# A graph layer on one core: the norms of the second and third pair of row blocks move by one product, and the first weight quarter is loaded in two parts

## The chip, the core and the metric

The kernel runs on one core of a Trainium2 chip. The metric is device time in microseconds (us), the median of several runs. The engines are named as in the profile: PE is TensorE, which does the matmuls (PEld is its weight load); DVE is VectorE; ACT is ScalarE; POOL is GpSimd; SP is SyncE, which only issues DMAs here. ACT and POOL issue DMAs as well.

## What is computed

The reference normalises each row of x, applies a relu, and runs a relational graph convolution with a highway gate on the result. Cut to what matters:

```python
h = jnp.maximum(_layernorm(x, axis=-1), 0.0)      # x: 1250 x 1024, float32
u = h @ root + bias
for r in range(8):                                # 20000 edges, 8 types
    mean_r = (sum of h[src] over the edges of type r into each row) / max(count, 1)
    u = u + mean_r @ weight[r]                    # 1024 x 1024 each
z = concatenate([u, h], axis=1) @ w_gate + b_gate
out = x + tanh(u) * z + h * (1.0 - z)
```

## The kernel before

**Blocks and steps.** The 1250 rows are ten blocks of 128 (the last has 98). `NP` is 5, and blocks i and i + 5 form pair i. The kernel multiplies h with all eight `weight[r]`, with `root` and with the two halves of `w_gate`, and gathers the products row by row later. A step (s, i) multiplies pair i with matrix s. Steps run over i inside s.

**A step is seven products.** A pair has 2 x 2 quarters of the left side (A11, A12 from the first block, A21, A22 from the second), and the matrix has 2 x 2 quarters of 512 x 512 (`b11`, `t3` at first, `b21`, `b22`). The step uses Winograd's form of Strassen's scheme with seven products. `left` makes the sums S1, S2, S4 and S3 on DVE, and `make_t1` to `make_t4` (L167, L171, L175, L179) make the right sides, also on DVE. Each product is four `k`-blocks of 128 rows, in float32, which the profile shows as eight matmuls of L292. For the first matrix the order of the products is A11, S1, S2, S4 (`p3`), S3 (`p7`), A12 (`p2`), A22, except in the step (0, 0), where A12 comes directly behind A11. The products use two PSUM banks `b` and `c` in turn. ACT copies them out behind A11 (L330), S1 (L337), S2 (L341, called the sixth product in the code), S3 (L316) and A22 (L359). DVE adds behind S4 (L309), S3 (L317) and A12 (L325). The copies matter for order: S2 and S3 accumulate into the bank that L330 and L341 read, and S4 into the one that L337 reads.

**The norm.** The input of a pair is loaded into SBUF (L560). `both` normalises the two blocks: statistics and scale factors on DVE (L579, L583, L588, L589), a square root on ACT (L584), and the scaled relu on ACT (L605). `store` writes h to DRAM (L610). `with_x` adds x and h on DVE and stores the sum (L615, L616). `factored` and `transposed` then transpose h on PE (L259) and copy the result out on ACT and DVE (L266, L264) to be the left side. The first pair is done ahead of all products in a shorter way (L598, L262); `second_block` does its second half behind the first product.

**Order of the work beside the products.** Every engine works through its instructions in the order in which the program writes them; there is no scheduler that changes it (`manual_schedule`). After each product the kernel calls `done()`, which calls `between`, which advances a generator `index()` by one `yield`. So a `yield` more or less moves all that follows in the generator by one product, on all engines. `index()` runs `norms()` and `columns()` side by side, one `yield` each per product, with `norms()` first. `columns()` makes the edges' keys on DVE (L709 to L721 behind the seventh product, L728 to L741 one product later), and transposes them on PE (L748, L749). When both have ended, `slots` gives each edge its place in a table, in 40 chunks of two `yield`s (small matmuls L802 and L853 on PE, L784 and L786 on ACT, L807 and others on DVE, scatters L881 on POOL), and `order` sorts the rows and loads the table back (L935 on DVE, L527, L537, L490 on POOL). From step (4, 0) on, `weights` (L513 to L519) and the gathers (L1061, L1069) work with that table.

**Loads.** x and the first matrix are loaded through SP's queue, except the right halves of x's blocks 0 and 5, which go through ACT's queue. The order on SP today is x(0), x(5), `b11`, `b21`, `t3`, `b22` (all L135 but x), then the second and third pair of x. `b11` is 1 MiB.

Of the kernel before, what the change touches and what calls it, by code (L numbers as in the profile page):

```python
# [19 lines left out]
def tile_rgcn_highway(  # L20
# [35 lines left out]
    P = 128  # L56
# [4 lines left out]
    KQ = KC // 2  # L61
    Q = D // 2
# [27 lines left out]
    def nrows(d):  # L90
        return min(P, N - d * P)
# [34 lines left out]
    class Factors:  # L126
# [3 lines left out]
        def __init__(self, w, old=None):  # L130
            self.w, self.old = w, old

        def load(self, i, j, to, queue=None):
            queue = queue or (nc.scalar if self.old else nc.sync)
            queue.dma_start(to, self.w[i * Q:(i + 1) * Q, j * Q:(j + 1) * Q]  # L135
                            .rearrange("(k p) n -> p k n", p=P))
            return to

        def load_first(self):
            old = self.old  # L140
            if old is None:
                free = wbuf
                self.place = dict(b11=free[0], t3=free[1], b22=free[2], t1=free[3], t2=free[4],
                                  b21=free[5], t4=free[6])
                self.spare = free[7:]
            else:
                p = old.place
                self.place = dict(b11=old.spare[0], t3=old.spare[1], b22=p["b11"], t1=p["t1"],
                                  t2=p["t2"], b21=p["b22"], t4=p["t3"])
                self.spare = [p["b21"], p["t4"]]  # L150
            p = self.place
            self.of = {A11: p["b11"], A12: p["b21"], S4: p["b22"], S1: p["t1"], S2: p["t2"],
                       S3: p["t3"], A22: p["t4"]}
            self.load(0, 0, p["b11"])

        def load_next(self):
            self.load(0, 1, self.place["t3"], nc.sync)
# [23 lines left out]
    class Second:  # L181
# [22 lines left out]
        def left(self):  # L204
            nc.vector.tensor_add(self.s1, self.a21, self.a22)
            nc.vector.tensor_sub(self.s2, self.s1, self.a11)
            nc.vector.tensor_sub(self.s3, self.a11, self.a21)
            nc.vector.tensor_sub(self.s4, self.a12, self.s2)
# [43 lines left out]
    def transposed(aop, part, of, n, relu=False):  # L252


        for half, to in enumerate(((A11, A12), (A21, A22))[part]):
            p = bank().rearrange("p (k f) -> p k f", k=KQ)
            for i in range(KQ):
                k = KQ * half + i
                nc.tensor.transpose(p[:, i, :n], of[:n, k * P:(k + 1) * P], ident[:n, :n])  # L259
            to_n, p_n = aop[:, to, :, :n], p[:, :, :n]  # L260
            if half and relu:
                nc.vector.tensor_scalar_max(to_n, p_n, 0.0)  # L262
            elif half:
                nc.vector.tensor_copy(to_n, p_n)  # L264
            else:
                nc.scalar.activation(to_n, p_n, AF.Relu if relu else AF.Copy)  # L266
            if n < P:
                nc.gpsimd.memset(aop[:, to, :, n:], 0.0)
# [103 lines left out]
    fac = []  # L372
# [173 lines left out]
    with ExitStack() as early:  # L546
# [6 lines left out]
        def load_x(i, part, t=None, pieces=1):  # L553
            d = i + part * NP
            n = nrows(d)
            if t is None:
                t = xpool.tile([P, D], F32, name="xt")
            for j in range(pieces):
                at = slice(j * D // pieces, (j + 1) * D // pieces)
                (nc.scalar if j else nc.sync).dma_start(t[:n, at], x[d * P:d * P + n, at])  # L560
            return t

        def scratch(i, part):

            return h_op[i][:, 2 * part:2 * part + 2].rearrange("p a k f -> p (a k f)")
# [52 lines left out]
        def both(a, b):  # L618

            a.stats(0)  # L620
            a.stats(1)
            a.spread()
            b.stats(0)
            a.scale()
            a.relu()
            b.stats(1)
            b.spread()
            b.scale()
            b.relu()

        def factored(i, blocks):
            for part in range(2):
                transposed(h_op[i], part, blocks[part].ht, blocks[part].n)


        warm = xpool.tile([P, 1], F32, name="warm")
        x0 = [load_x(0, part, pieces=2) for part in range(2)]
        nc.scalar.activation(warm, eps, AF.Sqrt)
        fac[0].load_first()
        fac[0].load_b21()  # L640
        fac[0].load_next()
        fac[0].load_b22()
# [307 lines left out]
                    yield  # L950

        def norms():
            yield
            yield
            both(*b1)
            fac[0].make_t4()
            for b in b1:
                b.store()
            yield
            yield  # L960
            yield
            factored(1, b1)
            left(h_op[1])
            yield
            for b in b0:
                b.with_x()
            x3 = [load_x(3, part) for part in range(2)]
            b2 = [Normed(2 + part * NP, x2[part], scratch(NP - 1, part)) for part in range(2)]
            both(*b2)
            yield  # L970
            for b in b2:
                b.store()
            yield
            for b in b1:
                b.with_x()
            yield
            factored(2, b2)
            b2[0].with_x(b2[0].ht)
            b2[1].with_x()
            left(h_op[2])  # L980
            x4 = [load_x(4, 0)]
            yield
            yield
            b3 = [Normed(3 + part * NP, x3[part], scratch(NP - 1, part)) for part in range(2)]
            both(*b3)
            yield
            for b in b3:
                b.store()
            yield
            factored(3, b3)  # L990
            left(h_op[3])
            yield
            for b in b3:
                b.with_x()
            x4.append(load_x(4, 1))
            yield
            for part in range(2):
                ht = xpool.tile([P, D], F32, name="xt") if part else scratch(NP - 1, 1)
                b = Normed(4 + part * NP, x4[part], ht)
                b.stats(0)  # L1000
                b.stats(1)
                b.spread()
                b.scale()
                b.relu()
                b.store()
                yield
                transposed(h_op[4], part, b.ht, b.n)
                b.with_x()
                yield
            left(h_op[4])  # L1010
            first_part.close()
# [11 lines left out]
        while going[0]:  # L1023
            s, i = next(steps)
# [11 lines left out]
    with ExitStack() as edges_part:  # L1036
# [44 lines left out]
        def edges(g, blocks, to, late=0):  # L1081

            of = u_dram[g - 1] if g else None
            nb = len(blocks)
            starts = [late + sum(K[g][d] for d in blocks[:b]) for b in range(nb + 1)]
            leaves = [starts[b + 1] - 1 + GOT for b in range(nb)]
            reads = [max(-1, starts[b] - 5, leaves[b - UB] if b >= UB else -1) for b in range(nb)]  # L1090
            u, then = {}, {}
            for t in range(-1, leaves[-1] + 4):
                for b, d in enumerate(blocks):
                    if starts[b] <= t < starts[b + 1]:
                        k = t - starts[b]
                        add_slot(u[d], g, d, k, idx[:, g], w_of[:, g], first=g == 0 and k == 0)
                for b, d in enumerate(blocks):
                    if t == leaves[b]:
                        then[t + 3] = to(d, u[d])
                if then.get(t):  # L1100
                    then[t]()
                for b, d in enumerate(blocks):
                    if t == reads[b]:
                        u[d] = new_u(d, of, g)
                yield
# [49 lines left out]
        def beside(e, total, s, i, last):  # L1155


            between = spread(e, total, 7 * ((last - s) * NP + NP - i))
            while s <= last:
                step(s, i, between)  # L1160
                s, i = next(steps, (NM, 0))
            return s, i

        s, i = next(steps)
        while s <= R0[1]:
            step(s, i)
            s, i = next(steps)
# [8 lines left out]
        def with_others(e):  # L1176

            others = other_groups()
            for k, _ in enumerate(e):
                yield  # L1180
                if k % 2:
                    next(others, None)
            for _ in others:
                pass

        weights(0)
        s, i = beside(with_others(edges(0, range(ND), u_back(0))), sum(K[0]) + 2, s, i,
                      R0[2] - 1)
# [6 lines left out]
        for g in range(1, G - 1):  # L1195
# [3 lines left out]
            s, i = beside(e, sum(K[g]) + LATE + 1, s, i, R0[g + 2] - 1)  # L1199
# [153 lines left out]
        while s < NM - 1:  # L1353
# [8 lines left out]
            s, i = next(steps, (NM, 0))  # L1362

        for i in range(NP):
# [55 lines left out]
            else:  # L1420
                product(h_op[i % 2], fac[NM - 1], t, between=beside_last, last=finish_last,
                        pieces=2, second=lambda: None,
# [24 lines left out]
```

## Time and profile before

| what | value |
|---|---|
| median of 3 runs | 1368.39 us (1367.49 to 1369.36) |
| the profiled execution's own time | 1366.53 us |
| its span, from first to last instruction | 1364.7 us |
| mean granted TensorE clock | 1.000 |
| busy: PE, DVE, POOL, ACT | 1349.9, 932.9, 638.8, 365.7 us |
| products in float32 (L292) | 2800 matmuls, 593 ns each |

A line of a group of instructions or of the timeline names the engine, the line in the source, the operation, the tiles written and read, and the count; in brackets stands how long the engine was idle before it and which instruction ended that. The view of waits sums the same by pair of waiting and releasing line. A copy that is late does not show as a wait of the copying engine, when that engine was busy with something else: it shows as a wait of PE for that copy.

### The profile page before, as it was taken

Reading aid. Unit: us, or ns where it says so; the run is one execution under the profiler, and the core shown is the slowest. Engines: PE = TensorE matmul, PEld = TensorE weight load, DVE = VectorE, ACT = ScalarE, POOL = GpSimd, SP = SyncE. Lnnn points to the kernel's source line nnn. Section 1 sums busy time; section 2 is a strip of 40 time slices with the busy share of each in tenths; the row PEclk is TensorE's granted clock in tenths of the full one; section 3 lists DMA queues with packets and bytes.
Section 4 is the critical chain, followed back from the end, with each engine's and each line's share of the span. In section 5 each row is a group of like instructions: output and inputs, shape, how many; then the busy total and the mean of one; then the engine's idle time right before and its main releaser. Section 6 shows DMA issues by size and latency. Waiting matters only on the chain.

```text
span 1364.7 us, 12816 instructions
## 1 busy us (share of the span) xinstructions
PE 1349.9 (99%) x3810; PEld 659.9 (48%) x3810; DVE 932.9 (68%) x1849; ACT 365.7 (27%) x792; POOL 638.8 (47%) x571
## 2 busy tenths in 40 slices
PE   8999999999999999999999999999999999999998
PEld 4444455455445544544554454455445445544443
DVE  6855887887885946567565756765664586567985
ACT  3235566566631111111111111111111111121220
POOL 0002655665561464557774435465443344435641
PEclk9999999999999999999999999999999999999999
DMA  8654565855663175379788627787965664586861
GB/s 312 253 196 131 121 139 134 191 115 114 158 167 93 61 206 137 116 250 254 218 282 315 213 81 287 264 303 258 347 217 201 217 239 149 194 284 219 294 205 58
DMA packets 110202, 272.77 MB, mean 200 GB/s; under 512 B 25956, under 2 KB 27986, under 8 KB 110000
## 3 DMA queue, kind: packets, MB, share of 16 engines
q0 software_dynamic: 48912, 128.60, 29.5%
q1 hardware_dynamic: 45088, 111.34, 26.3%
q10 hardware_dynamic: 16128, 31.98, 7.9%
q8 instruction: 30, 0.49, 0.2%
q14 instruction: 44, 0.36, 0.1%
HBM read 214.20 MB, written 80.65 MB: 216 GB/s over the span
## 4 chain that ended last, share of the span: by engine, by line
PE 91%; issue 4%; DVE 2%; POOL 1%; DMA 1%; ACT 0%; SPq 0%; POOLq 0%; DVEq 0%; ACTq 0%
PE ps L292 82%; PE ps L212 8%; PE ps L259 1%; PE ps_n L802 1%; DMA w<-in_L_gnn_weight_dram 1%; POOL out_dram L496 1%; DVE h_op L275 0%; PE ps_q L853 0%; POOL got L490 0%; DMA xt<-in_x_dram 0%; DVE st L579 0%; DMA xh_dram<-xt 0%; DVE h_op L615 0%; DVE w L171 0%; DVE h_op L264 0%
## 5 line engine op out<-in xcount | busy, mean ns | idle before, releaser
L292 PE MATMUL ps<-w,h_op 128*128 128x512 f32 x2800 | 1224.5, 593 | 6.2 <-ACT row L341 2.6
L292 PEld LDWEIGHTS ps<-w,h_op 128*128 128x128 f32 x2800 | 526.6, 190 | 620.2 <-issue 601.5
L1061 POOL DMA_INDIRECT got<-y,idx x202 | 256.0, 1267 | 265.7 <-DVE u L1069 197.2
L1069 DVE SCALAR_TENSOR_TENSOR u<-got,w_of,u 128x1024 f32<-128x1024 f32 (+1 forms) x192 | 246.0, 1283 | 127.6 <-DMA got<-y,idx 125.1
L881 POOL DMA_INDIRECT table<-row_col,at_i x157 | 180.2, 1148 | 154.1 <-DVE at_i L877 73.3
L317 DVE TENSOR_TENSOR row<-row,part 128x512 f32<-128x512 f32 x55 | 38.0, 690 | 109.6 <-ACT part L316 109.6
L359 ACT COPY row<-ps 128x512 f32<-128x512 f32 x50 | 29.3, 585 | 239.0 <-PE ps L292 234.1
L316 ACT COPY part<-ps 128x512 f32<-128x512 f32 x55 | 32.2, 585 | 179.8 <-PE ps L292 176.6
L309 DVE TENSOR_TENSOR row<-row,ps 128x512 f32<-128x512 f32 x54 | 36.9, 684 | 57.3 <-PE ps L292 53.3
L330 ACT COPY row<-ps 128x512 f32<-128x512 f32 x55 | 32.2, 586 | 163.2 <-PE ps L292 163.2
L337 ACT COPY row<-ps 128x512 f32<-128x512 f32 x55 | 32.2, 586 | 147.9 <-PE ps L292 144.3
L212 PE MATMUL ps<-w,w 128*128 128x256 f32 x288 | 71.3, 380 | 0.0
L341 ACT COPY row<-ps 128x512 f32<-128x512 f32 x55 | 32.2, 586 | 139.3 <-PE ps L292 139.3
L212 PEld LDWEIGHTS ps<-w,w 128*128 128x128 f32 x288 | 54.4, 190 | 20.9 <-issue 15.3
L807 DVE TENSOR_TENSOR seen<-seen,ps_n 128x110 f32<-128x110 f32 x157 | 42.1, 268 | 25.1 <-PE ps_n L802 20.8
L867 DVE SCALAR_TENSOR_TENSOR junk<-k_bc,key_col,before 128x128 f32<-128x128 int32 x157 | 54.9, 350 | 4.2
L527 POOL DMA_INDIRECT node_dram<-ids,pos_i x30 | 37.4, 1247 | 43.2 <-issue 42.9
L212 PE MATMUL ps<-w,h_op 128*128 128x256 f32 x216 | 56.0, 382 | 0.0
L935 DVE SCALAR_TENSOR_TENSOR junk<-v_bc,val,one 128x1280 bf16<-128x1280 f32 x30 | 46.6, 1554 | 9.5 <-DMA v_bc<-val_dram 8.7
L212 PEld LDWEIGHTS ps<-w,h_op 128*128 128x128 f32 x216 | 40.5, 190 | 25.3 <-issue 22.2
L784 ACT ACTIVATE is_lo<-io,less_lo 128x128 bf16<-128x128 f32 x157 | 50.1, 391 | 4.8 <-DMA xh_dram<-xt 4.8
L490 POOL DMA_INDIRECT u<-u_dram,node x20 | 22.9, 1145 | 51.3 <-DMA last_dram<-u 34.9
(187 smaller groups left out, 957.8 us busy)
## 6 DMA issues: line engine op xcount, KB each, us to landing
y<-row SPq DMA_DIRECT2D x72, 512.0 KB, 5.6
w<-in_L_gnn_weight_dram ACTq DMA_DIRECT2D x21, 1024.0 KB, 10.1
w<-in_L_gnn_weight_dram SPq DMA_DIRECT2D x11, 1024.0 KB, 13.3
k_bc<-keys_dram SPq DMA_DIRECT2D x39, 256.0 KB, 4.2
l_bc<-los_dram SPq DMA_DIRECT2D x39, 256.0 KB, 8.4
w<-in_L_gnn_w_gate_dram ACTq DMA_DIRECT2D x6, 1024.0 KB
h_dram<-h_op SPq DMA_DIRECT2D x9, 512.0 KB, 2.9
hr_dram<-row SPq DMA_DIRECT2D x9, 512.0 KB, 6.7
```

Source lines behind the costliest of these rows:

```text
L212: nc.tensor.matmul(p, a[:, k, :], b[:, k, :], start=(fresh and k == 0), stop=(k == 1), skip_group_check=True)
L292: nc.tensor.matmul(b[:, at], aop[:, i, k, :], w.of[i][:, k, at], start=(fresh and k == 0), stop=(k == KQ - 1), skip_group_check=True)
L309: nc.vector.tensor_add(c12, c12, c)
L317: nc.vector.tensor_add(c22, c22, d)
L527: ins = nc.gpsimd.indirect_dma_start(out=node_dram[g][:, :], out_offset=bass.IndirectOffsetOnAxis(ap=pos_i[:, g, d:d + 1], axis=0), in_=id ...
L784: nc.scalar.activation(is_lo[:, i, :], io, AF.Abs, bias=less_lo[:, c0 + i:c0 + i + 1])
L807: nc.vector.tensor_add(seen[j][:, i, :], was, p[:, i, :])
L867: nc.vector.scalar_tensor_tensor(junk, o["k_bc"][:, i, :], key_col[:, c:c + 1], before, op0=OP.is_equal, op1=OP.mult, accum_out=rank[:, c: ...
L881: ins = nc.gpsimd.indirect_dma_start(out=table[:, :], out_offset=bass.IndirectOffsetOnAxis(ap=at_i[:n, i:i + 1], axis=0), in_=row_col[:n, ...
L935: nc.vector.scalar_tensor_tensor(junk, v_bc[:, g, :], val[:, c:c + 1], one.to_broadcast([P, KEYS]), op0=OP.is_gt, op1=OP.mult, accum_out=p ...
L1061: nc.gpsimd.indirect_dma_start(out=t[:n], out_offset=None, in_=y[g][:, :], in_offset=bass.IndirectOffsetOnAxis(ap=at[:n, d, k:k + 1], axis=0),
L1069: nc.vector.scalar_tensor_tensor(u[:n], t[:n], w, u[:n], op0=OP.mult, op1=OP.add)
```

## The change

Three edits to the order, none to what is computed. First, `load` and `load_first` get a parameter `k`, and `b11` is loaded in two DMAs of two `k`-blocks each, the first in front of block 5 of x, the second behind it. Second, in `norms()` one `yield` moves from behind the second pair's norm to in front of it, so that it stands behind S2 instead of S1 in step (0, 0). Third, there is one more `yield` behind the first pair's `with_x`, so that the loads of the fourth pair's x and the third pair's norm come behind A11 of step (0, 1), and one more between the norm and the transposes of each block of the last pair. `norms()` has 22 `yield`s instead of 19.

```diff
-        def load(self, i, j, to, queue=None):
+        def load(self, i, j, to, queue=None, k=slice(0, KQ)):
             queue = queue or (nc.scalar if self.old else nc.sync)
-            queue.dma_start(to, self.w[i * Q:(i + 1) * Q, j * Q:(j + 1) * Q]
+            queue.dma_start(to[:, k], self.w[i * Q + k.start * P:i * Q + k.stop * P,
+                                             j * Q:(j + 1) * Q]
                             .rearrange("(k p) n -> p k n", p=P))
...
-        def load_first(self):
+        def load_first(self, k=slice(0, KQ)):
...
-            self.load(0, 0, p["b11"])
+            self.load(0, 0, p["b11"], k=k)
...
-        x0 = [load_x(0, part, pieces=2) for part in range(2)]
+        x0 = [load_x(0, 0, pieces=2)]
+        fac[0].load_first(slice(0, 2))
+        x0.append(load_x(0, 1, pieces=2))
         nc.scalar.activation(warm, eps, AF.Sqrt)
-        fac[0].load_first()
+        fac[0].load(0, 0, fac[0].place["b11"], k=slice(2, KQ))
...
         def norms():
-            yield
-            yield
+            for _ in range(3):
+                yield
             both(*b1)
             fac[0].make_t4()
             for b in b1:
                 b.store()
             yield
             yield
-            yield
             factored(1, b1)
             left(h_op[1])
             yield
             for b in b0:
                 b.with_x()
+            yield
             x3 = [load_x(3, part) for part in range(2)]
             b2 = [Normed(2 + part * NP, x2[part], scratch(NP - 1, part)) for part in range(2)]
             both(*b2)
...
                 b.store()
+                yield
                 yield
                 transposed(h_op[4], part, b.ht, b.n)
                 b.with_x()
```

## The prediction

> **What bounds the kernel now.** I read the page's busy shares first, then TensorE's waits, then the timeline of the first 50 us, where nearly all of these waits lie. All times are those of the profiled execution.
>
> ```profile
> PE 1349.9 (99%) x3810; PEld 659.9 (48%) x3810; DVE 932.9 (68%) x1849; ACT 365.7 (27%) x792; POOL 638.8 (47%) x571
> ```
>
> TensorE is busy 99% of the span, so only what makes it stand still, or gives it more work, can move the time. The view of TensorE's waits (releaser: us in total, times, longest):
>
> ```profile
> PE ps L292 <- ACT row L341: 2.6, 1, 2.6
> PE ps L292 <- ACT row L330: 1.6, 1, 1.6
> ...
> PE ps L292 <- DMA w<-in_L_gnn_weight_dram: 1.3, 1, 1.3
> PE ps L259 <- ACT xt L605: 0.8, 1, 0.8
> ...
> PE ps L748 <- DVE h_op L264: 0.5, 1, 0.5
> ```
>
> Five waits, 6.8 us together, each once. The same view from 130 us to the end has one line, 0.7 us on "issue". So 6.8 us (0.5%) is the most that this change can gain, and the question is which of the five it removes and what it puts there. The timeline (start, duration, then in brackets the idle time before it and its releaser):
>
> ```profile
> 7.46 0.60 ACT L266 ACTIVATE h_op<-ps 128x512 f32<-128x512 f32 x1 [1.59 <-PE ps L259]
> 9.16 3.67 PE L292 MATMUL ps<-w,h_op 128*128 128x512 f32 x8 [1.28 <-DMA w<-in_L_gnn_weight_dram]
> ...
> 13.54 13.90 PE L292 MATMUL ps<-w,h_op 128*128 128x512 f32 x32
> ...
> 14.35 1.22 DVE L167 TENSOR_TENSOR w<-w,w 128x1024 f32<-128x1024 f32 x1
> ...
> 28.19 2.28 DVE L179 TENSOR_TENSOR w<-w,w 128x2048 f32<-128x2048 f32 x1
> 28.31 1.24 ACT L605 ACTIVATE h_op<-h_op,less,rs 128x1024 f32<-128x1024 f32 x1 [0.42 <-DVE less L589]
> ...
> 29.46 0.56 ACT L341 COPY row<-ps 128x512 f32<-128x512 f32 x1
> ...
> 30.08 3.70 PE L292 MATMUL ps<-w,h_op 128*128 128x512 f32 x8 [2.63 <-ACT row L341]
> ...
> 41.36 1.27 DVE L579 BATCH_NORM_STATS2 st<-h_op 128x6 f32<-128x512 f32 x2
> ...
> 46.77 0.56 ACT L330 COPY row<-ps 128x512 f32<-128x512 f32 x1
> ...
> 47.39 2.84 PE L292 MATMUL ps<-w,h_op 128*128 128x512 f32 x6 [1.57 <-ACT row L330]
> ```
>
> See the 2.63 us: the 32 matmuls from 13.54 are A12, S1, S2, S4, 3.44 us each, so S2 ended near 23.9. Its copy L341 stands on ACT behind the second pair's norm, whose last activation ends at 29.5, and S3 needs the bank that L341 reads. The 1.57 us is the same with the third pair's norm in front of L330. The 1.28 us is TensorE waiting for the first quarter `b11` although its left side (L266) was ready at 8.06.
>
> **The change part by part.** I lay out the new order on the old clock.
>
> *Start.* SP's queue becomes x(0), half of b11, x(5), other half. The windows view has 379 to 412 GB/s from 6 us on; all of x(0), x(5) and b11 (2.1 MB) landed at 9.03 (the chain: issue 1.67 plus 7.36). The last half MiB takes 1.3 us of that, x(5)'s SP piece 0.65, so the first half lands near 6.5 to 7, x(5) near 7.3 to 7.6, the second half still near 9.1. A11 then starts when L266 is done, at 8.15 instead of 9.16; its third k-block comes 1.75 us later, at 9.9, so the second half has 0.8 us to spare. Gain: 1.0 us. The price is x(5): its stats (L579) began at 7.03 and would begin up to 0.6 later; its first relu piece (now 9.76 to 10.5) then ends near 11.1, and its transposes are wanted at 11.66: covered. [...] The windows row of this trace:
>
> ```profile
> 8.00:9.00 1.00, 0.00 (x0) 0.00 (x0) 1.00 (x3) 0.06 (x1) 0.00 (x0) 1.00 1.03 397
> ```
>
> In the last microsecond of the wait the engines are full at 397 GB/s with several loads queued. [...] I take the row. [...]
>
> *After A11.* A12 starts at 12.5, S1 could at 15.97. S1 needs the first half of t1 (L167) and its left sum (L275). L167 needs t3, two MiB after b11: 9.03 + 2 x 2.6 (1.05 MB at 404 GB/s), about 14.2. So VectorE starts L167 at 14.2, only 0.15 earlier than now, and S1 starts at 16.05. Then S2 19.5, S4 22.9, S3 26.4.
>
> *Second pair's norm one product later.* VectorE has no instruction between S1 and S2, so its order does not change: stats still from 24.1, t4 (L179) until 30.3. Only ACT changes: L341 now stands before the norm and runs at 23.0 to 23.6, and behind it the issue of the next matrix's first load (0.39 us in this trace), both before the sqrt at 25.65. S3 starts at 26.4 without a wait: the 2.63 us is gone. What is late next: the transposes behind S3 (29.9) need both relus, which end at 27.7 and 29.55; covered by 0.3 to 1.3 us. A22 follows at 31.65 (t4 ready at 30.3) instead of 35.36: 3.7 earlier.
>
> *Third pair's norm in the next step.* Now A11 and L330 of step 1 come before this norm, so L330 is free and the 1.57 us goes. In exchange the norm stands behind `columns()`'s first part on VectorE, and in front of its second part and of L337. VectorE from t4 on, without a pause: L309 and L317 1.2, two transposed copies 1.25, left sums 2.74, L615 twice 2.35, casts and keys L709 to L721 2.5: 40.2 to 40.6. Norm on VectorE 4.23 (41.36 to 45.59 now): 44.4 to 44.8. L728 to L741, 2.74 (48.41 to 51.15 now): tb ready at 47.2 to 47.5. TensorE ends S2 of step 1 at 45.65, and the next instruction in its queue is now the transpose of key, row and tb (L748), because the sixteen transposes of the third pair, which stand before it today, have moved behind S4. Its own work is 1.34 (1.82 less the 0.48 wait), so S4 could start at 47.0, but tb lets it start at 47.7 to 48.05: a new wait of 0.7 to 1.05, in place of 1.57 and 0.48. L337 (after the norm's relus, 40.4 + 5.5 = 45.9, so done by 46.6) is earlier than that and hides. Compare S4's start: now 54.50 with the 1.75 us of transposes before it, that is 52.75; then 47.7 to 48.05: 4.7 to 5.05 gained. VectorE sets this point from 14.2 on, so the 1.0 us of the start is mostly swallowed here.
>
> *The last norm and the rest.* The extra yield puts the last block's transposes behind A11 of step 3, two products after its norm, where ACT's relu (now 87.87 to 89.1) is long done: the 0.85 us goes. The fourth pair's norm now sits after A12, its transposes after the next A11; relus end near 67.4, the second block's transposes stand at 68.0: 0.6 us of cover. Sum: 4.7 to 5.05 plus 0.85, 5.6 us.
>
> *What moves on the queues.* On SP the x(3), x(8) loads fall behind four key stores and two y stores, issued near 42.5 against 43.0 now, and wanted at 62; the next matrix's second load moves ahead of two h stores and is wanted 80 us later; the xh stores stay with L615. `norms` has 22 yields instead of 19, so all slots and the ordering come three products later. ACT's first L784 stays behind the landing of the last xh store (4.8 us idle today, hidden by L342's one product of slack). On POOL the scatters L881 and the chain L527, L537, L490 shift by 3 x 3.6 = 10.8 us against the products: the last idx load at 490.3 is wanted by `weights(0)` at 516.2, and the gathers' first four buffers, issued by 505.5, at 524.9. Both keep over 8 us even with some landing time; without that cover each us over would hold VectorE and then TensorE. The index part now ends in step (3, 4) instead of (3, 3), still before step 4. TensorE's instructions are the same, so I cost them at nothing.
>
> Unknown: how the slots' small matmuls fall between the products after a shift by an odd number of products. From one side, 40 chunks (157 columns of edges by four) with no wait in some 300 us today: nothing. From the other, weight loads waiting for L786 0.2 us four times: if each chunk did so, 8 us lost; in favour, up to 0.7 ("issue"). I take nothing, the nearer row: two products per chunk and seven per step bring either alignment in the kernel of today as well.
>
> The profiled execution took 1366.53 (span 1364.7), 1.9 below the median; taking 5.6 off gives 1360.9 on that execution and 1368.39 - 5.6 = 1362.8 for the median.
>
> **The rivals.** *The wait comes back (chance 0.14).* Norm, columns and transposes meet on VectorE between 30 and 48 us. For it: VectorE is busy throughout and L337 waits for the norm. If this stretch runs 2.5 us longer than added up, S4 starts at 50.4 and the gain is 3.1: 1365.3; about half of this case falls within 0.2%. Against: every term is a measured duration.
>
> *The slots lose step (0.10): slower.* L802 and L853 wait for ACT's L786 and L837 at the new alignment. From 5.6/40 = 0.14 us per chunk the gain is gone, from 0.21 it is slower by over 0.2%; at 0.3 it is 12 us: 1374.8. For: VectorE and ACT are more than half full there. Against: no such wait today.
>
> *It does not do what it says (0.04).* If S3 were really held by another releaser than L341 and the split bought nothing: 1368.4. Against: the copy starts within 0.1 us of the norm's last relu ending, and S3 within 0.1 us of the copy's end.
>
> **How the numbers follow.** Likeliest (0.72): 1362.8, on its own 1361.3 (all waits gone, 6.8) to 1364.5. The range goes to 1367.0, so that it holds most of the first rival, and down to 1361.0. 0.2%, 2.7 us, is about what a measurement of this kernel can tell from no change. Faster by more: 0.72 and half of 0.14, with a little for tails: 0.80; same: 0.10; slower: 0.10.
>
> **What would show it.** Right: A11 starts near 8.2; no wait on L341, L330 or L605; a new wait of about 1 us on TensorE at L748 for VectorE's row or tb; S4 of step 1 near 48; still none after 130. Wrong: A11's third block waiting for its half; the x(5) transposes waiting; a wait on L337; waits at L802 or L853; w_of waiting for idx near 511.

## The result, and the profile after

| | before | after |
|---|---|---|
| median of 7 runs, same chip | 1368.39 us (1367.49 to 1369.90) | 1364.05 us (1362.83 to 1364.52) |
| ratio, 95% interval | | 0.9965 (0.9954 to 0.9977) |
| profiled execution, its span | 1366.53, 1364.7 us | 1364.05, 1362.3 us |

The change made the kernel 4.3 us (0.35%) faster; 1362.8 was forecast. Two later comparisons gave 7.8 and 5.9 us for the same two kernels; what makes these differ is taken up below. One execution, of the kernel with the filled hole, ran at about half the clock throughout (mean clock 0.556, 2410 us) and is left out of that kernel's median. Lines of the source are a few higher after the change (L292 is L293, L341 is L342, L748 is L751).

First the busy shares of the page of after, then its view of TensorE's waits (waiting line, releaser: us in total, times, longest):

```profile
PE 1350.3 (99%) x3810; PEld 659.9 (48%) x3810; DVE 932.0 (68%) x1849; ACT 365.4 (27%) x792; POOL 639.8 (47%) x571
```

```profile
PE ps_q L856 <- ACT s_b L840: 1.4, 1, 1.4
...
PE ps L293 <- ACT row L342: 1.0, 1, 1.0
PE ps L751 <- DVE row L742: 0.9, 1, 0.9
PE ps L293 <- issue: 0.7, 1, 0.7
PE ps L260 <- DVE h_op L599: 0.7, 1, 0.7
...
```

TensorE has the same 3810 instructions. Of the five waits that the prediction listed none is left. In their place stands the 0.9 us on L742. The first and the 1.0 us line are new too, and they lie elsewhere: L342 here is at 180 us and L840 at 358 us, in the slots part (the expectations below put the latter near 405 us). The timeline of the start, TensorE alone (start, duration, in brackets the idle time before it and its releaser):

```profile
8.28 3.70 PE L293 MATMUL ps<-w,h_op 128*128 128x512 f32 x8 [0.23 <-ACT h_op L267]
12.04 1.36 PE L260 MATMUL ps<-ident,h_op 128*128 128x128 f32 x8
13.24 17.62 PE L293 MATMUL ps<-w,h_op 128*128 128x512 f32 x40
30.70 1.91 PE L260 MATMUL ps<-ident,h_op 128*128 128x128 f32 x16
32.45 13.90 PE L293 MATMUL ps<-w,h_op 128*128 128x512 f32 x32
...
47.49 0.33 PE L751 MATMUL ps<-ident,row 128*128 128x128 f32 x1 [0.86 <-DVE row L742]
...
48.35 3.70 PE L293 MATMUL ps<-w,h_op 128*128 128x512 f32 x8
```

Where 32 matmuls stood before the 2.63 us hole, 40 now run without one (13.24: A12, S1, S2, S4, S3), and S4 of step (0, 1) starts at 48.35. The same stretch on VectorE and ScalarE:

```profile
8.43 1.28 DVE L580 BATCH_NORM_STATS2 st<-xt 128x6 f32<-128x512 f32 x2 [1.15 <-DMA xt<-in_x_dram]
...
14.92 1.22 DVE L168 TENSOR_TENSOR w<-w,w 128x1024 f32<-128x1024 f32 x1 [0.79 <-DMA w<-in_L_gnn_weight_dram]
...
24.04 0.59 ACT L342 COPY row<-ps 128x512 f32<-128x512 f32 x1 [2.85 <-PE ps L293]
...
47.01 0.43 DVE L742 TENSOR_TENSOR row<-row,late 128x256 f32<-128x256 f32 x1
```

L342 runs at 24.04, before the norm instead of behind it. But L168 now has an idle 0.79 us in front of it, released by a DMA; in the profile before it started at 14.35 with no wait.

Where the gain is kept and lost is best seen by counting. All kernels have the same 2800 large matmuls in nearly the same order, so the start of the n-th one in before (counted from 0), less its start in another kernel, is the gain up to there (both from the traces):

```
n-th matmul   at (before)    after   after on the chip of the third comparison
    48          35 us         2.9      2.9
   176         100 us         5.5      5.5
   300         156 us         5.9      5.8
   400         210 us         5.0      6.1
   700         363 us         3.1      5.8
  1000         506 us         2.45     5.2
 2799 (last)  1359 us         2.45     5.2
```

The rows between 176 and 1000 need care. The small matmuls of the slots (L805 and L856) begin behind the 183rd large one in before and three products later in after, so at 300 after has done eight of them fewer, worth 0.4 us, and does them by the end of the slots. At 176 and at 1000 both kernels have done the same work. So the change earned 5.5 us in the first 100 us, as worked out, and in the profiled execution on record 3.1 of it was lost again by 506 us: 0.25 on the third chip as well, and 2.8 with the two late waits (2.4 of it listed as idle time).

### The profile page after: what moved, and what is told of

It is laid out like the page before. It is cut to its first block, busy times and chain, and to the rows that moved or that the text cites. A ratio compares the mean times of both kernels' runs of the same rounds, so it can differ in the third digit from the quotient of the medians.

```text
span 1362.3 us, 12814 instructions
## 1 busy us (share of the span) xinstructions
PE 1350.3 (99%) x3810; PEld 659.9 (48%) x3810; DVE 932.0 (68%) x1849; ACT 365.4 (27%) x792; POOL 639.8 (47%) x571
## 4 chain that ended last, share of the span: by engine, by line
PE 90%; issue 4%; DVE 2%; DMA 2%; POOL 1%; SPq 1%; ACT 0%; POOLq 0%; DVEq 0%; ACTq 0%
PE ps L293 80%; PE ps L213 8%; DMA xt<-in_x_dram 1%; PE ps L260 1%; DMA w<-in_L_gnn_weight_dram 1%; PE ps_n L805 1%; POOL out_dram L497 1%; SPq L561 0%; PE ps_q L856 0%; DVE u L1276 0%; POOL got L491 0%; DVE h_op L276 0%; DVE row L1377 0%; DVE h_op L1323 0%; DVE h_op L1340 0%
## 5 line engine op out<-in xcount | busy, mean ns | idle before, releaser
L293 PE MATMUL ps<-w,h_op 128*128 128x512 f32 x2800 | 1224.4, 593 | 2.0 <-ACT row L342 1.0
L293 PEld LDWEIGHTS ps<-w,h_op 128*128 128x128 f32 x2800 | 526.5, 190 | 615.6 <-issue 600.6
L1065 POOL DMA_INDIRECT got<-y,idx x202 | 259.8, 1286 | 243.7 <-DVE u L1073 189.6
L884 POOL DMA_INDIRECT table<-row_col,at_i x157 | 176.6, 1125 | 160.9 <-DVE at_i L880 74.5
L213 PE MATMUL ps<-w,w 128*128 128x256 f32 x288 | 71.3, 380 | 0.0
L342 ACT COPY row<-ps 128x512 f32<-128x512 f32 x55 | 32.2, 586 | 139.0 <-PE ps L293 133.3
L213 PEld LDWEIGHTS ps<-w,w 128*128 128x128 f32 x288 | 54.4, 190 | 20.9 <-issue 15.3
L213 PE MATMUL ps<-w,h_op 128*128 128x256 f32 x216 | 56.0, 382 | 0.0
L213 PEld LDWEIGHTS ps<-w,h_op 128*128 128x128 f32 x216 | 40.5, 190 | 25.6 <-issue 22.1
```

Source lines behind the costliest of these rows:

```text
L213: nc.tensor.matmul(p, a[:, k, :], b[:, k, :], start=(fresh and k == 0), stop=(k == 1), skip_group_check=True)
L293: nc.tensor.matmul(b[:, at], aop[:, i, k, :], w.of[i][:, k, at], start=(fresh and k == 0), stop=(k == KQ - 1), skip_group_check=True)
L884: ins = nc.gpsimd.indirect_dma_start(out=table[:, :], out_offset=bass.IndirectOffsetOnAxis(ap=at_i[:n, i:i + 1], axis=0), in_=row_col[:n, ...
L1065: nc.gpsimd.indirect_dma_start(out=t[:n], out_offset=None, in_=y[g][:, :], in_offset=bass.IndirectOffsetOnAxis(ap=at[:n, d, k:k + 1], axis=0),
```

## The experiments

The kernels of one comparison ran on one chip, each comparison on another; their medians are compared with that chip's own runs of before: first comparison 1367.53 us (1365.89 to 1370.15, 18 runs), second 1372.73 (1368.83 to 1375.31, 17 runs), third 1367.29 (1366.00 to 1368.18, 9 runs).

### One part at a time

**The first yield alone** (before, and only this):

```diff
-            yield
-            yield
+            for _ in range(3):
+                yield
             both(*b1)
...
             yield
             yield
-            yield
             factored(1, b1)
```

> The kernel before with one edit: one yield moves from behind the second pair's norm to in front of it (norms keep 19 yields, the later stages keep their places). Theory (the copy behind S2 is held by that norm on ScalarE): the 2.6 us wait for it goes; the third pair's norm still holds the copy behind A11 of step (0, 1), so a wait of some 1.3 us for it stays, and the 0.5 us at the key transposes and the 0.85 us at the last block's transposes stay. S4 of step (0, 1) near 51.5 instead of 54.5, time about 3 us less: 1365.4. Rival (the split of b11 and the later yields carry the gain): under 1 us less.

Measured: 1363.53 us (1363.01 to 1365.78), ratio 0.9973 (0.9963 to 0.9984), 4.0 us less; about 3 was expected. S4 of step (0, 1) starts at 51.23. In the trace the gain is 3.27 us by the 48th matmul (the 2.63 us, and 0.6 because A11 waited 0.7 us for `b11` in this profile instead of 1.28) and 3.17 at the end; L330's 1.57 us and L605's 0.85 stay, and there is no late wait. With the other yields, but no split, 6.4 us was gained on this chip (below), so this one line is most of the change.

**The split load alone** (before, with `b11` in two loads around x(5)):

```diff
-        x0 = [load_x(0, part, pieces=2) for part in range(2)]
+        x0 = [load_x(0, 0, pieces=2)]
+        fac[0].load_first(slice(0, 2))
+        x0.append(load_x(0, 1, pieces=2))
...
-        fac[0].load_first()
+        fac[0].load(0, 0, fac[0].place["b11"], k=slice(2, KQ))
```

> The kernel before with the split of b11 around block 5 of x, and no yield moved. Theory (from the load of t3 on, VectorE sets the pace): A11 starts near 8.3 instead of 9.16, but L167 for t1 starts at 14.9 instead of 14.35 because the loads land 0.6 us later, so the second pair's norm and the 2.6 us wait behind it end 0.5 us later: 0 to 0.6 us slower than before, 1368.4 to 1369. Rival (the prediction's start term): 1.0 us faster, 1367.4.

Measured: 1368.96 us (1367.18 to 1370.27), ratio 1.0009 (1.0000 to 1.0018): 1.4 us more in the median, hardly clear of no change, where the prediction's term for the start gives 1.0 less. A11 did start early, at 8.04. But t1 moved from 14.35 to 14.98, and with it the norm and the copy that S3 waits for, so the early microsecond of TensorE turned up again as a longer wait. The timeline and the windows view (the column after the busy times is the granted clock; the last two are the DMA share and GB/s) of this kernel:

```profile
30.72 6.72 PE L293 MATMUL ps<-w,h_op 128*128 128x512 f32 x8 [3.23 <-ACT row L342]
```

```profile
27.00:31.00 4.00, 0.77 (x3) 0.28 (x2) 3.28 (x6) 3.14 (x4) 0.00 (x0) 0.88 0.81 288
31.00:34.00 3.00, 3.00 (x4) 1.22 (x5) 0.71 (x2) 0.00 (x0) 0.00 (x0) 0.50 0.88 240
34.00:38.00 4.00, 4.00 (x12) 1.86 (x11) 0.00 (x0) 0.53 (x2) 0.00 (x0) 0.65 1.03 393
```

The wait is 3.23 us instead of 2.63, and S3 took 6.72 us instead of 3.70, because the granted clock was 0.50 from 30.0 us on, for 6.83 us. The prediction had no such cost of a wait; the section on the hardware comes back to it.

**The two yields without the split** (after, with the loads of before):

```diff
-        x0 = [load_x(0, 0, pieces=2)]
-        fac[0].load_first(slice(0, 2))
-        x0.append(load_x(0, 1, pieces=2))
+        x0 = [load_x(0, part, pieces=2) for part in range(2)]
...
-        fac[0].load(0, 0, fac[0].place["b11"], k=slice(2, KQ))
+        fac[0].load_first()
```

> The changed kernel with all its yields, but block 5 of x before the whole of b11, as in the kernel before. Theory: A11 starts at 9.16 again, L167 at 14.35, and as VectorE sets the start of S4 of step (0, 1), that is at 47.8 instead of 48.35: 0.3 to 0.6 us faster than the changed kernel. Rival: the split is worth its 1.0 us, and without it the time is 1.0 us more than the changed kernel's.

Measured: 1361.14 us (1360.78 to 1361.49), ratio 0.9953 (0.9939 to 0.9967). Its timeline, TensorE and VectorE:

```profile
9.12 3.67 PE L293 MATMUL ps<-w,h_op 128*128 128x512 f32 x8 [1.30 <-DMA w<-in_L_gnn_weight_dram]
...
14.31 1.22 DVE L168 TENSOR_TENSOR w<-w,w 128x1024 f32<-128x1024 f32 x1
```

A11 waits its 1.30 us for `b11` again, t1 is back at 14.31, and S4 of step (0, 1) starts at 48.27. With the split it starts at 48.35 in the trace on record, and at 48.69 in the next kernel, on the same chip as this one. At the point where everything meets, the split is worth nothing, or costs some 0.4 us. This kernel had no late waits, and neither had the next one, which suggested that the parity of the shift (22 yields or 23) or the split caused them.

**One more yield at the end of the norms** (after, so that the slots move by an even number of products):

```diff
             left(h_op[4])
+            yield
             first_part.close()
```

> The changed kernel with one more yield at the end of norms, so that the chunks of the slots come four products later than before instead of three. Theory (the two waits after 130 us, 1.4 us for the cast of s_b and 1.0 us for the copy behind S2, come from the odd shift: in a step where two done() stand with only a few small matmuls between them, the cast now falls before the short gap and the placing behind it): with the even shift each chunk meets the steps as in the kernel before, no wait for s_b at the 405 us place, time 1 to 2.4 us less than the changed kernel. Rival (those waits are chance of one execution, or come from starting earlier): same time, waits of 1 to 2.4 us still there.

Measured: 1361.68 us (1361.24 to 1362.54), ratio 0.9958 (0.9944 to 0.9972), S4 at 48.69, no late wait over 0.7 us. That fitted parity, but after itself had not run on this chip.

### The same chip for both

**After once more:**

> The changed kernel once more, beside the next three on the same chip. Theory (the waits of 1.0 and 1.4 us after 130 us belong to this kernel in every execution, and not only to one): median 1363.5 to 1364.5 and the same two waits in its profile. Rival (chance of one execution): without them, 1361.5 to 1362.

Measured: 1364.91 us (1364.40 to 1365.94), ratio 0.9945 (0.9928 to 0.9961), 7.8 us below a before that was 5 us slower here. The late waits are there, 1.6 us (L840) and 1.2 us (L342), in front of the same two large matmuls as on record, the 352nd and the 696th (counted from 0).

**The first quarter in two loads, both behind x(5)** (after, with the order of before):

```diff
-        x0 = [load_x(0, 0, pieces=2)]
-        fac[0].load_first(slice(0, 2))
-        x0.append(load_x(0, 1, pieces=2))
+        x0 = [load_x(0, part, pieces=2) for part in range(2)]
         nc.scalar.activation(warm, eps, AF.Sqrt)
+        fac[0].load_first(slice(0, 2))
```

> The changed kernel with b11 in two loads, but both behind block 5 of x. Theory A (one more boundary between loads on SP's queue costs the 0.6 us): A11 starts 0.5 to 1 us earlier than in the kernel before (8.2 to 8.6), and t1's first half (L168) still waits for t3 until 14.9. Theory B (the order around block 5 costs it): A11 at 8.2 to 8.6, L168 at 14.3, block 5's statistics at 7.0 again. Under both S4 of step (0, 1) is at 48.2 to 48.4, where TensorE's products up to the second pair's transposes and then VectorE set it, and the time is within 0.5 us of that without the split, apart from the late waits.

Measured: 1364.39 us (1364.23 to 1366.27), ratio 0.9940 (0.9924 to 0.9956). TensorE and VectorE in its timeline:

```profile
8.88 3.67 PE L293 MATMUL ps<-w,h_op 128*128 128x512 f32 x8 [0.98 <-DMA w<-in_L_gnn_weight_dram]
...
15.27 1.23 DVE L168 TENSOR_TENSOR w<-w,w 128x1024 f32<-128x1024 f32 x1 [1.12 <-DMA w<-in_L_gnn_weight_dram]
```

x(5) is in its old place, A11 still waits 0.98 us, and t1 is late all the same, at 15.27. Over all traces t1 starts at 13.88 to 14.35 in the seven kernels' traces with `b11` in one load, and at 14.92 to 15.27 in the seven with two. So it is not the order around x(5) that delays the loads behind, but that there is one load more (the order with both halves behind x(5) has one trace). This profile, of the slowest of the six runs, has three late waits, 1.6, 1.3 and 1.2 us.

**The columns one product later, no split** (against the new wait on L742; from the kernel without the split):

```diff
-            for _ in range(6):
+            for _ in range(7):
                 yield
             for name in ("dst", "typ", "src"):
```

> The changed kernel without the split, and with columns() one product later (7 yields in front instead of 6), so that the norm of the third pair stands on VectorE before the keys, and the key transposes stand behind S4 of step (0, 1). Theory (the new 0.8 to 0.9 us wait of TensorE for row is VectorE's order at that place): that wait goes, S4 starts near 46.2, 0.8 us less than the kernel without the split: 1360.3. Rival (VectorE's sum of work sets the pace, in whatever order): the wait comes back at another line, the same time.

Measured: 1364.05 us (1363.06 to 1365.30), ratio 0.9938 (0.9921 to 0.9955), 0.9 us below after on this chip, though the two kernels' runs overlap. In its timeline the second run of 40 has no hole:

```profile
31.98 17.33 PE L293 MATMUL ps<-w,h_op 128*128 128x512 f32 x40
```

The last block's transposes stand at 92.63 us against 94.07 in after. The two late waits stayed (1.6 and 1.3 us) although there is no split here, so they do not need the split.

**The hole of before filled with work** (before, with ten 128x128 products of the identity between S4 and S3 of step (0, 0), whose result is not used):

```diff
             between(j)
+            if (s, i, j) == (0, 0, 4):
+                p = bank()[:, :P]
+                for _ in range(10):
+                    nc.tensor.matmul(p, ident, ident, start=True, stop=True)
```

> The kernel before with ten matmuls of the identity put behind S4 of step (0, 0), in the 2.6 us in which TensorE waits for the copy behind S2; their result is not used. Theory (in part of the executions of the kernel before, this wait lets the granted clock fall to a half for some 7 us, as it did in the profile of the split alone from 30.0 to 36.8): no execution falls, mean granted clock 0.999 or more in all, and the times lie within 1 us of each other near 1366.3, while the kernel before beside it spreads to 1370. Rival (the spread has another cause): the same spread and median as the kernel before.

Measured: 1370.24 us, the median of eleven runs (1368.55 to 1372.47), ratio 0.9986 (0.9973 to 0.9998): 2.5 us less in the median, although work was added. S3 starts at 29.90 behind a wait of 0.42 us. None of these runs had a mean clock below 0.998, while 8 of the 17 of before had 0.996 or 0.997. That speaks for the clock as part of the price of a hole. But the spread did not close to the 1 us that was expected: in the profile the clock halved elsewhere, at 188.84 us, for 3.41 us:

```profile
187.55 5.40 PE L292 MATMUL ps<-w,h_op 128*128 128x512 f32 x8 [2.09 <-issue]
```

The product took 5.40 us instead of 3.70, and with the wait this place cost 4.1 us against the trace of before. The wait stands in front of the 352nd large matmul, where the first late wait of after stands, but in a kernel with the order of before and no yield moved. The one trace of before, from the comparison on record, does not have it.

### The third chip

**After, the kernel without the split, and the one with the even shift, again, side by side:**

> The changed kernel once more, now on the same chip as the versions without the split and with the even shift beside it. Theory (its two waits after 130 us are its own): 2 to 3 us over both of them, with a wait of TensorE for s_b near 405 us. Rival (they belong to the chip of the run): no such waits in any of the three, or in all.

> The changed kernel without the split of b11 again, odd shift as in the changed kernel. Theory A (the odd shift costs the late waits): they are here too, and the time is within 0.5 us of the changed kernel's, because S4 of step (0, 1) starts at 48.3 in both. Theory B (the split costs them): no late wait, 2 to 3 us less than the changed kernel, as the medians of two different chips said.

> The changed kernel with one more yield at the end of norms (even shift) again. Theory A (odd shift): no wait for s_b, 1.5 to 2.5 us less than the changed kernel beside it. Theory B (the split): the same late waits as the changed kernel, same time.

Measured: 1361.37 us (1361.29 to 1361.59), 1361.26 (1360.84 to 1363.63) and 1361.24 (1361.03 to 1362.53); ratios 0.9959 (0.9945 to 0.9972), 0.9965 (0.9952 to 0.9979) and 0.9961 (0.9947 to 0.9975). All three are the same. From 130 us on, after's waits of TensorE here are one line:

```profile
PE ps L293 <- issue: 0.7, 1, 0.7
```

The same kernel has 2.4 and 2.8 us of late waits in two of its three profiles and none in the third. The odd shift alone does not bring them (three profiles with it, this one and both of the kernel without the split, have none), and the first one also came with no shift at all, in the filled kernel. Whether an even shift would avoid them where they appear is not shown: it did not run on the second chip. What the late copy itself looks like shows beside the same place here, first after on record, then here, ScalarE and TensorE:

```profile
179.75 0.59 ACT L342 COPY row<-ps 128x512 f32<-128x512 f32 x1 [2.21 <-PE ps L213]
178.36 1.03 PE L213 MATMUL ps<-w,w 128*128 128x256 f32 x4
```

```profile
178.62 0.59 ACT L342 COPY row<-ps 128x512 f32<-128x512 f32 x1 [1.02 <-PE ps L293]
178.42 1.03 PE L213 MATMUL ps<-w,w 128*128 128x256 f32 x4
```

The product that the copy reads stands right in front of L213, which starts at the same time in both to 0.1 us, and ScalarE is idle before the copy in both; yet on record the copy starts 1.1 us later.

**The best of all parts** (after without the split, with the columns one product later and the even shift):

```diff
-        fac[0].load(0, 0, fac[0].place["b11"], k=slice(2, KQ))
+        fac[0].load_first()
...
-            for _ in range(6):
+            for _ in range(7):
                 yield
...
             left(h_op[4])
+            yield
```

> All that the experiments point to together: the changed yields, no split, columns() one product later, and one more yield at the end of norms. If the new wait for row (0.8 us) and the wait for s_b (1.4 to 1.6 us) add up: 2.2 to 3 us less than the changed kernel beside it, no wait of TensorE over 0.5 us between A11 and the end but the 0.7 us on issue. Rival (one of the two comes back elsewhere): no better than the even shift alone.

Measured: 1359.60 us (1359.52 to 1359.68), ratio 0.9946 (0.9932 to 0.9959), 7.7 us below before and 1.8 below after on the same chip (2.2 to 3 was expected, with a wait for s_b that after does not have here). Its waits up to 130 us are two lines, then comes the timeline of the start:

```profile
PE ps L471 <- POOL eps L473: 1.4, 1, 1.4
PE ps L293 <- DMA w<-in_L_gnn_weight_dram: 0.8, 1, 0.8
```

```profile
8.70 3.67 PE L293 MATMUL ps<-w,h_op 128*128 128x512 f32 x8 [0.84 <-DMA w<-in_L_gnn_weight_dram]
...
13.08 17.33 PE L293 MATMUL ps<-w,h_op 128*128 128x512 f32 x40
30.25 1.91 PE L260 MATMUL ps<-ident,h_op 128*128 128x128 f32 x16
31.99 17.33 PE L293 MATMUL ps<-w,h_op 128*128 128x512 f32 x40
```

Two steps now run without a hole. The gain by the last matmul is 6.88 us; the wait for `b11`, 0.84 us, is what the split removes, and is still there.

## Why the prediction was right, and where it was off

**The second pair's norm: right.** The copy moved to 24.04, the 2.63 us went, and the first yield alone gave 3.2 us in the trace. S3 and A22 came at 27.27 and 32.45, not at 26.4 and 31.65: 0.8 to 0.9 late, nearly all of it from the start (A12 was 0.7 late).

**The start: A11 right, its price wrong.** A11 at 8.28 (8.15 said), and its third `k`-block did not wait (3.70 us for the product). Mis-sized was the landing of x(5) and of t3: x(5)'s statistics began at 8.43 (at most 7.6 said), so its transposes waited for L606 and A12 began 0.7 late; and L168 began at 14.92 behind its load (14.2 said). The windows view of before, and then of after, shows the reason:

```profile
4.00:5.00 1.00, 1.00 (x7) 1.00 (x6) 0.98 (x2) 0.00 (x0) 0.00 (x0) 1.00 1.02 381
5.00:6.00 1.00, 1.00 (x8) 1.00 (x8) 0.60 (x3) 0.29 (x1) 0.00 (x0) 1.00 0.91 287
6.00:7.00 1.00, 0.49 (x5) 0.33 (x4) 0.96 (x3) 0.00 (x0) 0.00 (x0) 1.00 1.00 379
```

```profile
4.00:5.00 1.00, 1.00 (x7) 1.00 (x6) 0.82 (x2) 0.00 (x0) 0.00 (x0) 1.00 0.78 223
5.00:6.00 1.00, 1.00 (x9) 1.00 (x8) 0.68 (x2) 0.25 (x1) 0.00 (x0) 1.00 0.78 231
6.00:7.00 1.00, 0.28 (x4) 0.12 (x3) 0.89 (x3) 0.04 (x1) 0.00 (x0) 1.00 0.84 279
```

In these 3 us before moved 1.05 MB and after 0.73; at 404 GB/s (after, 8 to 9 us) the missing 0.31 MB are 0.8 us, near the 0.6 us that t1 lost. The prediction took the row of 8 to 9 us of before, with a DMA share of 1.03 and 397 GB/s. The row held for the second half, which was in time. Yet the earlier start of A11 brought nothing at S4: side by side on the third chip, S4 started at 48.40 with the split and 47.95 without, and the medians were 1361.37 and 1361.26. One load more cost something between 4 and 7 us, where the DMA share of after is 0.78 to 0.84, and the prediction's rate was not taken from there. Why the rate is lower in those 3 us is not settled; that one more load suffices is what the two loads behind x(5) show. One candidate, not tested, is the issue: SP takes 0.4 to 0.6 us for each of these loads, and issues that of t3 at 3.28 instead of 2.69.

**The third pair's norm: right.** The new wait stands where it was put, at the key, row and tb transposes: 0.86 us (0.7 to 1.05 said), and S4 is at 48.35 (47.7 to 48.05), 0.3 to 0.65 late, as t1 was 0.7 late. The releaser is the second half of row, L742, one instruction ahead of tb. That VectorE sets this point was confirmed twice: the split moved A11 to an earlier start by 0.6 to 0.8 us, and S4 not; putting the columns one product later took this wait away.

**The last norm: right.** The 0.85 us is gone. By the 176th matmul, before the slots begin, the gain was 5.5 us; 5.6 was said. The parts were off by a little in opposite directions: S4 of step (0, 1), less the transposes, came 4.4 us earlier and not 4.7 to 5.05, and 1.1 us came after it instead of 0.85.

**The slots' alignment, costed at nothing: right to 0.25 us, without the late waits.** On the third chip, with no late wait, the gain is 5.5 us at the 176th matmul and 5.2 at the 1000th. The same 0.25 us goes in both traces without the split, 0.1 and 0.5 in the two with the even shift, and nothing in the best one or where only the first yield moved. So the small matmuls did not lose step, and "I take nothing" was nearly so.

**The late waits: not in the sum.** "Still none after 130" did not hold on record: TensorE waited once for L840 (the prediction had this wait as a rival, L853 for L837, but a little in each chunk) and once for L342 (not named), and lost 2.8 us. They come with the comparison, that is with the chip or with the time of the run, which were not separated, and not with the change alone: all four kernels traced on the second chip have a wait of 1.2 to 2.1 us in front of the 352nd large matmul, the filled kernel with the order of before among them; the traces of the first and the third chip have none there. Before's runs at a mean clock of 1.000 took 1366.0 us (median) on the third chip and 1369.0 on the second; all runs of after, at 0.999 or 1.000, took 1361.4 and 1364.9. So the second chip costs before 3.0 us and after 3.5. Why the copy starts later there stays open.

**Not in the sum: the clock.** The prediction priced a wait at its own length. On the third chip the medians differ by 5.9 us, but against before's runs at clock 1.000 (1366.0) after gains 4.7. The other 1.3 us are before's runs at 0.998, 5 of 9, with a median of 1367.7. On record, the profiled executions differ by 2.45 us where 5.6 was said, and the medians by 4.3, because before's median lies 1.9 us above its own profile, which ran at clock 1.000, and after's does not. (That the 1.9 us are the clock is argued from the other chips; the clocks of before's runs on record are not kept.) So it is luck in part that "1368.39 - 5.6" came within 1.3 us of the median: a loss of 2.8 us in the late waits and a gain of 1.9 us, both unforeseen, have opposite signs.

## What to carry to other kernels

Look for the one copy that stands behind a norm on a busy engine: moving the norm past it was worth 4.0 us of the 6.4 on the first chip, while the earlier start of the first product was worth nothing, because another engine set the next meeting point. A hole of TensorE can cost more than its length: here one of 2.09 us cost 4.1, and one of 3.23 us had 6.83 us at half clock with it, while the one of 2.63 us in the profile of before left the clock at 1.000. Price an additional load by what lands behind it. Compare variants on one chip before explaining a difference of 2 us by the variant: here the parity of a shift looked like the cause until after itself ran without the waits on a third chip. And count the gain between points at which both kernels have done the same work: work that is only put off looks like a gain, and later like a loss.

## What was not expected of the hardware

In two traces the granted clock fell to a half in or behind a hole of TensorE: in the split kernel at 30.0 us, inside the hole, for 6.83 us (0.50 in its windows view from 31 to 34 us), and in the filled kernel at 188.84, 1.3 us behind it, for 3.41 (0.50 from 189 to 192 us). In the traces every change of the granted clock lies a whole number of 3.413 us from the one before: in the split kernel 7 of them at full clock, then 2 at half; in the filled kernel 54, then 1 at half; in before and after 398 and 397 at full clock (1358.51 and 1355.09 us), and then the half behind the end of TensorE's work. A step of 3.413 us did not have to be idle as a whole: in the split kernel, TensorE idled 2.51 of the last 3.41 us before the drop; in the filled kernel 2.09; in the profile of before the hole put 1.98 us of idle time into one step, and there the clock stayed at 1.000. The ends of the traces agree, where TensorE stops for good inside a step: in eight of them that step had 2.21 us of idle time or more, and the clock was at half behind it; in the other six it had 1.88 or less (1.32 in before, 0.29 in after), and the clock was not. (Such an end holds up no matmul, but it shows in the mean clock: in the profile of after, with 0.999, the only drop is this one, 1.7 us before the end of the span.) If about 2.0 us of idle time in one step is the limit (an estimate from the 1.98 us without a drop and the 2.09 with one), and if a step can begin anywhere in the work, then where it begins decides: a hole of 2.63 us would halve the clock in about 60% of the executions, (2.63 + 3.41 - 2 x 2.0) / 3.41, and one of 3.23 us in about 77%. Of before's runs 8 of 18 on the first chip, 12 of 17 on the second and 5 of 9 on the third had a mean clock of 0.998 or less, 25 of 44 (57%); of the split kernel's, 8 of 11; of the filled kernel's, with its hole elsewhere, 2 of 11; of the kernel with the first yield alone, which keeps the 1.57 us hole, 1 of 8, which the estimate does not explain; of the 55 runs of after and its five variants, which have neither the 2.63 nor the 1.57 us, none. No profile of before itself caught the drop, so for before this is argued from the clocks of its runs, not seen in a trace.
